# Two of four gate/up units of a 4-bit FFN in three passes of 12-bit digits

## The chip, the cores and the metric

One Trainium2 chip, one NeuronCore of it. TensorE (PE) multiplies matrices, VectorE (DVE), ScalarE (ACT) and GpSimd (POOL) do the element-wise work, and SyncE (SP) issues every DMA of this kernel. Each engine runs its own instructions strictly in the order in which the program lists them, and they meet only in semaphores. The metric is device time in microseconds of one execution.

## The reference

The kernel computes four residual blocks on x of shape (2, 512, 256), each as x + layernorm(block(layernorm(x))):

```python
x = x + ln(softmax_attention(ln(x)))   # 16 heads of 128, rope, causal
x = x + ln(ffn4(ln(x)))                # 4-bit weights, hidden size 2048
x = x + ln(linear_attention(ln(x)))    # elu+1 features, cumulative sums
x = x + ln(ffn_lut(ln(x)))             # 16-entry table, hidden size 688

# ffn4; Wg, Wu, Wd = 4-bit codes -> LUT value * scale per 32 inputs
gate = einsum('th,nh->tn', xt, Wg)     # (1024,256) x (2048,256)
up   = einsum('th,nh->tn', xt, Wu)
gelu = tanh(0.79788 * (gate + 0.044715 * gate**3)) * gate * 0.5 + gate * 0.5
out  = einsum('tn,hn->th', gelu * up, Wd)
```

Everything is float32.

## The kernel before

The 1024 tokens are handled in four units u = 0 to 3 of 256 tokens (two units for each batch row). The program first runs the softmax attention of both rows in 34 slots, one for each of 32 (row, head) pairs and two to drain. Loads of weights, the expansion of the 4-bit codes (`dequantised`, L791, one of twelve jobs in every second slot) and the expansion of the 16-entry table weights of the last FFN are spread over the slots.

After attention come the four units of the 4-bit FFN. `ffn_hidden(u)` (L1089) makes eight steps, one for each pair of 128-row chunks of the hidden size. A step does eight products of 128 x 128 weights with 256 token columns: four for gate into a PSUM bank "mm", four for up into a bank "s" (two banks of each exist). ACT applies gelu to the gate bank (`ge`), DVE multiplies it with the up bank into `hT`. `ffn_out(u)` (L1117) then does 32 products of `hT` with the down weights into a bank "o". The outer loop (L1529 to L1534) runs what is left of hidden(u), then the first step of hidden(u+1), and then ffn_out(u). `hT` has two buffers, "hT" for even units and "hTb" for odd ones, so the first `hT` product of unit u+1 is made ahead of ffn_out(u).

When ffn_out(u) is done, a chain begins (`after_ffn`, L1134): the layer norms (`norms`, L411: statistics and scaled additions on DVE, powers on POOL, shifts on ACT, a block transpose on DVE with four DMAs), then `linear_attention(u)` (L1331: three projections on PE, Relu and Exp on ACT, running sums, products and reciprocals on DVE and POOL), then norms again. Its pieces are dealt out between the PE steps of the next unit. The last FFN follows: `silu_hidden(u)` and `silu_out(u)` for the four units.

A product goes through `matmul` (L277). From L1296 on `halved[0]` is true, and each 128 x 128 weight tile is issued as two tiles of 64 columns; the first few products of the program are issued whole. A float32 product shows two instruction records in the trace for each tile.

The order is written by a planner inside the program. `Engine` wraps DVE, ACT, POOL and SP, keeps an estimate of when each engine is free, and records each instruction at once (all show the line L183). Chains are polled after each PE step and advance when their estimated time has come. `select_in` (L469) turns table indices into weights in 19 DVE steps for each piece; the steps are kept in a queue of fills, and `fill` (L134) puts one ahead of another DVE instruction if it fits before that one's estimated start. `vector.flush()` puts all that are left at once. The down weights `wd` of the last FFN are made in this way from L1323 on, during the FFN units. The order on each engine is then fixed; a wrong estimate cannot change it when it runs.

Of the kernel before, what the change touches and what calls it, by code (L numbers as in the profile page):

```python
# [11 lines left out]
I32 = mybir.dt.int32  # L12
F8 = mybir.dt.float8e4
U8 = mybir.dt.uint8
SIGN = 0x80808080 - (1 << 32)
# [4 lines left out]
P = 128  # L20
HALF = P // 2
B = 2
S = 512
# [167 lines left out]
def sandwich_kernel(  # L191
# [85 lines left out]
    def matmul(out, lhsT, rhs, start, stop, beside=False, **more):  # L277
# [8 lines left out]
        times.add("PE", now[0], [out], [lhsT, rhs])  # L286

    def transpose(out, in_):
        nc.tensor.transpose(out, in_, ident)  # L289
        now[0] = max(now[0], times.start("PE", [out], [in_])) + 0.11  # L290
        times.add("PE", now[0], [out], [in_])
# [13 lines left out]
    sync.dma_start(out=cols_sb, in_=cols)  # L305
    cos_sb = const.tile([P, S], F32, name="cos_sb")
    sin_sb = const.tile([P, S], F32, name="sin_sb")
    bo_sb = const.tile([P, D], F32, name="bo_sb")
    lut_sb = const.tile([P, 16], F32, name="lut_sb")
# [223 lines left out]
    with ExitStack() as at:  # L533
# [4 lines left out]
        ac = at.enter_context(tc.tile_pool(name="ac", bufs=1))  # L538
        dq = at.enter_context(tc.tile_pool(name="dq", bufs=1))

        wts = {}
# [249 lines left out]
        def dequantised(packed, scales, u, name, w):  # L791
# [40 lines left out]

            def values():
                vector.scalar_tensor_tensor(
                    w,
                    c8.bitcast(F8),
                    64.0,
                    sc.unsqueeze(1).to_broadcast([P, 2, UNIT]),
                    ALU.mult,
                    ALU.mult,  # L840
                )

            behind.extend([lambda: scalar.copy(p8, pk), bits, values])

        jobs = deque()
        for u in range(NU):
            for src, sc, name, to in ((gate_p, gate_s, "g", wg_u), (up_p, up_s, "u", wu_u)):
                w = fw.tile([P, 2, UNIT], F32, name=f"w{name}{u}")
                jobs.append((src, sc, u, name, w))
                to.append(w)  # L850
# [224 lines left out]
        def after_attention(b):  # L1075
            yield 0.5
            for u in (2 * b, 2 * b + 1):
                xT1[u] = late.get("lw", acts).tile(
                    TURNED, F32, tag="xT1", name=f"xT1_{u}", bufs=2
                )  # L1080

                y = [half(acc, u)[:, j, :] for j in range(HT)]
                yield from norms(u, y, 1, xT1[u], strided=True)
            holder[0] = None


        hT1 = {}

        def ffn_hidden(u):  # L1089
            if u % 2 == 0:  # L1090
                hT1[u] = fh.tile([P, MLP // P, TU], F32, tag="hT", name=f"hT_{u}", bufs=1)
            else:
                hT1[u] = late["lw"].tile([P, MLP // P, TU], F32, tag="hTb", name=f"hT_{u}")
            nc_u = UNIT // P
            for c2 in range(0, MLP // P, 2):
                pg, pu = bank("mm"), bank("s")
                for ps, ws in ((pg, wg_u), (pu, wu_u)):
                    if ps is pu:
                        yield
                    for j in range(2):  # L1100
                        q, r = divmod(c2 + j, nc_u)
                        for kc in range(NK):
                            matmul(
                                ps[:, j * TU : (j + 1) * TU],
                                ws[q][:, kc, r * P : (r + 1) * P],
                                chunk(xT1[u], kc),
                                kc == 0,
# [9 lines left out]
        def ffn_out(u):  # L1117
            po = bank("o")
            for t in range(HT):
                for c in range(MLP // P):  # L1120
# [7 lines left out]
                    )  # L1128
                    if c % 2 and (t, c) != (HT - 1, MLP // P - 1):
                        yield  # L1130
            begin(after_ffn(u, po))
# [177 lines left out]

    lw = late["lw"] = ctx.enter_context(tc.tile_pool(name="lw", bufs=1))  # L1310
    lp = late["lp"] = ctx.enter_context(tc.tile_pool(name="lp", bufs=2))
    gp = ctx.enter_context(tc.tile_pool(name="gp", bufs=2))
# [7 lines left out]
    carry = {}  # L1320
    scratch = lw.tile([P, 8, 2 * D], F32, name="scratch2")
    vector.flush()
    select_in(  # L1323
        [scratch[:, j] for j in range(8)],
        [
            tuple(t[:, o : o + 2, :].rearrange("p o d -> p (o d)") for t in (down_i, wd))
            for o in range(0, NO, 2)
        ],
    )

    def linear_attention(u):  # L1331
# [22 lines left out]
        for part, e, f in ((1, ek, k), (0, eq, q)):  # L1354
            ps = project(part, "mm")
            scalar.activation(flat(e), ps, AF.Relu, scale=-1.0)
# [6 lines left out]
            else:  # L1363
                yield until(f)
        ps = project(2, "s")
        scalar.copy(flat(v), ps)
# [7 lines left out]
        yield until(k, v)  # L1374
        ks, kvs, den, lT = of("ks", 2), of("kvs", 2), of("den"), of("lT")

        def running_sum(to, of_):
            for ch in range(NK):
                before = carry[to is kvs, u - 1][:, ch, TU - 1 :] if u % 2 else 0.0
                vector.tensor_tensor_scan(  # L1380
                    to[:, ch, :], ones, of_[:, ch, :], before, ALU.mult, ALU.add
                )
            carry[to is kvs, u] = to

# [36 lines left out]

    hT2 = [lw.tile([P, NO, TU], F32, name=f"hT2_{j}") for j in range(2)]
    for t in hT2:
        pool.memset(t[:, FULL, :], 0.0)

    def silu_hidden(u):
# [12 lines left out]
        for o in range(0, NO, 2):  # L1439
            pg, pu = bank("mm"), bank("s")  # L1440
            for j in range(2):
# [7 lines left out]
                else:  # L1449
                    product(pg, at, wg, slice(FULL * P, FULL * P + 64 + REST))  # L1450
            si = gp.tile([P, 2 * TU], F32, tag="si", name="si")
            if o + 1 < FULL:
# [76 lines left out]
    for u in range(NUNIT):  # L1529
        run(hidden)  # L1530
        if u + 1 < NUNIT:
            hidden = ffn_hidden(u + 1)
            run(hidden, 2)
        run(ffn_out(u))  # L1534
    hidden = None
    vector.flush()
    for u in range(NUNIT):
        while u not in xT3:
# [100 lines left out]
```

## Time and profile before

| | |
|---|---|
| median of 3 runs | 618.06 us (617.79 to 618.41) |
| profiled execution, its span from first to last instruction | 616.7 us |
| the median less that span (start and end, outside the profile) | 1.4 us |
| PE busy | 611.1 us, 99% of the span |
| DVE, ACT, POOL busy | 486.2, 309.3, 277.1 us |
| attention, and what is hung on its slots, ends at about | 380 us |
| ffn_out of units 0, 1, 2, 3 begins at about | 390, 437, 486, 531 us |

A line of a group reads: source line, engine, operation, written tile <- read tiles, shapes, count | busy time in us, mean ns of one | idle time of the engine just before, and what ended it. A line of the timeline reads: start in us, duration in us, engine, line, operation, tiles, count; in brackets the idle time before it and what ended that. Shapes such as 128*64 128x256 on PE mean a weight tile of 128 rows and 64 columns, and 256 moving columns. The duration of a PE record contains its pipeline; the pace of PE is read from starts.

### The profile page before, as it was taken

The page shows a single profiled execution, that of the slowest core. Times are in us where ns is not written, and L with a number is a line of the kernel's source. Part 1 is how long each engine was busy: PE and PEld are TensorE (multiplying, and loading weights), DVE is VectorE, ACT ScalarE, POOL GpSimd, SP SyncE. Part 2 cuts the span into 40 slices and gives each one's busy share as a digit, 9 for nine tenths or more (in the row PEclk, how much of TensorE's full clock was granted, in tenths as well). Part 3 has the DMA queues.
Part 4 walks back from the last instruction along what each step waited for, and adds up shares of the span by engine and source line. Part 5 has one row for each costly group of instructions (what it writes and reads, how often), then busy time and mean ns, then how long its engine had stood idle before and what let it go on. Part 6 is the DMA issues. An engine that isn't in the chain of part 4 may idle for free.

```text
span 616.7 us, 13347 instructions
## 1 busy us (share of the span) xinstructions
PE 611.1 (99%) x4968; PEld 470.2 (76%) x4968; DVE 486.2 (79%) x1169; ACT 309.3 (50%) x716; POOL 277.1 (45%) x346
## 2 busy tenths in 40 slices
PE   9999999999999999999999999999999999999996
PEld 7455556566676776767777899999999999996665
DVE  7989988887887999989899789869986751562963
ACT  6657776775666657676566651232324223325210
POOL 5355657454453575855667300350261350161531
PEclk9999999999999999999999999999999999999999
DMA  8477474765647547556552340211001000001010
GB/s 228 137 186 211 107 199 125 171 168 144 158 127 177 168 116 191 152 142 178 113 141 60 84 104 26 98 35 35 1 8 31 1 18 18 1 2 35 19 53 18
DMA packets 44463, 61.43 MB, mean 100 GB/s; under 512 B 5232, under 2 KB 32368, under 8 KB 44400
## 3 DMA queue, kind: packets, MB, share of 16 engines
q1 hardware_dynamic: 44400, 60.59, 38.0%
q8 instruction: 39, 0.64, 0.4%
q14 instruction: 24, 0.20, 0.1%
HBM read 28.59 MB, written 1.05 MB: 48 GB/s over the span
## 4 chain that ended last, share of the span: by engine, by line
PE 98%; DVE 1%; issue 0%; POOL 0%; DVEq 0%
PE ps_mm L282 40%; PE ps_o L282 22%; PE ps_s L282 21%; PE ps_t L282 14%; PE ps_o L579 1%; DVE x L183 0%; DVE p L183 0%; DVE rr L183 0%; DVE ra L183 0%; DVE centred L183 0%; POOL rstd L183 0%; DVE wg L183 0%; PE ps_t L289 0%; DVE st L183 0%; DVE st_last L183 0%
## 5 line engine op out<-in xcount | busy, mean ns | idle before, releaser
L183 DVE SCALAR_TENSOR_TENSOR rr<-ps_mm,cols_sb,sin_sb 64x512 f32<-64x512 f32 (+1 forms) x126 | 93.4, 741 | 3.6 <-PE ps_mm L282 0.7
L183 POOL TENSOR_TENSOR wg<-wg,scratch 128x752 f32<-128x752 f32 x30 | 53.8, 1794 | 89.3 <-DVE scratch L183 86.9
L282 PE MATMUL ps_mm<-xT,wg 128*64 128x256 f32 (+1 forms) x704 | 89.4, 379 | 0.0
L282 PE MATMUL ps_s<-xT,wu 128*64 128x256 f32 x672 | 85.4, 379 | 0.0
L183 ACT ACTIVATE p<-p,mn 128x512 f32<-128x512 f32 (+3 forms) x128 | 70.3, 550 | 27.6 <-DVE mn L183 27.6
L282 PE MATMUL ps_o<-wd,hT 128*64 128x256 f32 (+1 forms) x704 | 77.2, 375 | 0.0
L282 PE MATMUL ps_t<-pT,v 128*64 128x256 f32 (+3 forms) x512 | 76.1, 432 | 0.0
L282 PEld LDWEIGHTS ps_mm<-xT,wg 128*64 128x64 f32 (+1 forms) x704 | 71.7, 137 | 5.5 <-ACT si L183 0.4
L282 PEld LDWEIGHTS ps_o<-wd,hT 128*64 128x64 f32 x704 | 68.9, 137 | 6.2
L282 PEld LDWEIGHTS ps_s<-xT,wu 128*64 128x64 f32 x672 | 69.5, 137 | 4.5 <-DVE hT L183 0.3
L282 PEld LDWEIGHTS ps_t<-pT,v 128*64 128x64 f32 x512 | 49.7, 137 | 27.1 <-issue 19.0
L183 ACT ACTIVATE p<-p,rs 128x512 f32<-128x512 f32 (+3 forms) x128 | 61.4, 551 | 11.2 <-DVE rs L183 9.3
L282 PEld LDWEIGHTS ps_o<-wo,oT 128*64 128x64 f32 x512 | 49.9, 137 | 17.8 <-issue 13.3
L282 PE MATMUL ps_o<-wo,oT 128*64 128x256 f32 x512 | 62.5, 379 | 0.0
L282 PE MATMUL ps_mm<-xT,wq 128*64 128x512 f32 (+2 forms) x256 | 60.5, 577 | 0.1
L282 PE MATMUL ps_mm<-xT,wk 128*64 128x512 f32 x248 | 60.0, 592 | 0.0
L183 POOL TENSOR_TENSOR ra<-ra,cos_sb 128x512 f32<-128x512 f32 (+1 forms) x33 | 41.1, 1245 | 40.2 <-ACT ra L183 38.4
L282 PE MATMUL ps_s<-kT,qT 128*64 128x64 f32 (+5 forms) x384 | 57.0, 424 | 0.0
L282 PE MATMUL ps_mm<-wv,xTv 128*64 128x256 f32 x464 | 56.4, 379 | 0.0
L183 DVE STREAM_TRANSPOSE turned<-p 128x512 f32<-128x512 f32 (+3 forms) x128 | 54.1, 480 | 1.2 <-ACT p L183 0.2
L183 ACT ACTIVATE ln<-x,shift,rstd 128x256 f32<-128x256 f32 x22 | 13.3, 607 | 79.0 <-POOL shift L183 78.2
L282 PEld LDWEIGHTS ps_s<-kT,qT 128*64 128x64 f32 x384 | 34.6, 137 | 23.9 <-issue 11.6
(161 smaller groups left out, 965.3 us busy)
## 6 DMA issues: line engine op xcount, KB each, us to landing
pT<-turned SPq DMA_DIRECT2D x128, 208.0 KB, 3.9
wo<-in_wo SPq DMA_DIRECT2D x17, 256.0 KB, 4.2
wv<-in_wv SPq DMA_DIRECT2D x16, 256.0 KB, 4.2
wq<-in_wq SPq DMA_DIRECT2D x15, 256.0 KB, 4.2
wk<-in_wk SPq DMA_DIRECT2D x15, 256.0 KB, 4.0
xT<-tr SPq DMA_DIRECT2D x48, 64.0 KB, 2.1
pk_g<-in_gate_p SPq DMA_DIRECT2D x4, 256.0 KB, 4.6
sc_g<-in_gate_s SPq DMA_DIRECT2D x8, 128.0 KB, 4.2
```

The costliest lines, as they stand in the source:

```text
L183: return write(*args, **more)
L282: nc.tensor.matmul(out[part], lhsT=lhsT[:, part], rhs=rhs, start=start, stop=stop, **more)
L579: nc.tensor.matmul(warm[:, :P], lhsT=units, rhs=units, start=True, stop=True)
```

## The change

The gate and up products of units 2 and 3 are done on numbers of type float32r, split into parts of 12 bits. A weight w has a top part (its upper bits, by a bit mask), and w = top + the rest; a token x is split alike. A product then takes three passes: weights as they are with tokens as they are, `low` with `low`, `dif` with `dif`, where `low` and `dif` are sums and differences of the parts scaled by powers of 4096. Between the second and the third pass ACT multiplies the PSUM bank by 1 + 1/4096 in place.

What this adds or moves, by place:

- `ffn_hidden_in_digits` takes the place of `ffn_hidden` for units 1 to 3. It is a pipeline: passes 1 and 2 of the next pair are issued ahead of pass 3 of this one. Unit 1 keeps float32 products in it, units 2 and 3 use digits.
- `split_weights` cuts one 128 x 512 piece of gate or up weights: a mask on DVE, a subtraction on POOL (`low`), and at the next call a scaling on ACT and a second subtraction on POOL (`dif`). There are 16 pieces and two buffers for the masked part. It is called after each step of units 1 to 3 and three times in each half of ffn_out(u), u > 0, once the norms of the second row are through. With the first piece of the last quarter it also calls `vector.flush()`.
- `split_tokens` makes the two extra token tiles of units 2 and 3: three DVE operations and one on ACT.
- `hT` has one buffer for all units, so no `hT` product of unit u+1 can stand ahead of ffn_out(u).
- `halved[0]` becomes false after attention, so that all products of the rest are issued whole.
- The expanded gate and up weights go to a staging tile `wt` and are copied into place by a DMA of 512 KB, eight in all, during attention.
- Linear attention projects into banks "t" in place of "mm" and "s", keeps its carries in small tiles, and writes over its inputs where it had own tiles before. Several constants and `hT2` share room with other tiles.

```diff
@@ new helper
+    def digits(out, lhsT, rhs, first):
+        nc.tensor.matmul(out, lhsT=lhsT, rhs=rhs, start=first, stop=False, skip_group_check=True)
+        now[0] = max(now[0], times.start("PE", [out], [lhsT, rhs])) + 0.117
+        times.add("PE", now[0], [out], [lhsT, rhs])
...
@@ dequantised
             def values():
+                to = w if name == "d" else dq.tile([P, 2, UNIT], F32, tag="wt", name=f"wt_{name}{u}")
                 vector.scalar_tensor_tensor(
-                    w,
+                    to,
...
+                if to is not w:
+                    sync.dma_start(out=w.bitcast(F32), in_=to)
...
+        def split_tokens(u):
+            x = xT1[u].bitcast(F32)
+            top = fh.tile(TURNED, F32, tag="ge", name=f"top_{u}")
+            low, dif = (
+                late["lw"].tile(TURNED, F32R, tag=f"x{n}", name=f"x{n}_{u}", bufs=2) for n in ("low", "dif")
+            )
+            vector.tensor_scalar(top.bitcast(I32), x.bitcast(I32), TOP, None, ALU.bitwise_and)
+            vector.scalar_tensor_tensor(dif, top, -1.0 - 1.0 / RADIX, x, ALU.mult, ALU.add)
+            vector.scalar_tensor_tensor(low, dif.bitcast(F32), RADIX, top, ALU.mult, ALU.add)
+            scalar.mul(dif, dif.bitcast(F32), RADIX)
+            x3[u] = xT1[u], low, dif
+
+        def ffn_hidden_in_digits(u):
+            hT1[u] = fh.tile([P, MLP // P, TU], F32, tag="hT", name=f"hT_{u}", bufs=1)
...
+            def begun_(kind, n):
+                ps = banks_of[kind, n] = bank(("mm", "s")[kind])
+                if in_digits(n):
+                    passes(kind, n, (0, 1))
+                    scalar.mul(ps, ps, 1.0 + 1.0 / RADIX)
+                    return
...
+            def ended(kind, n):
+                if in_digits(n):
+                    passes(kind, n, (2,))
+                ps = banks_of.pop((kind, n))
+                if kind == 0:
+                    ge_of[n] = fh.tile([P, 2 * TU], F32, tag="ge", name="ge")
+                    scalar.activation(ge_of[n], ps, AF.Gelu_apprx_tanh)
+                else:
+                    to = hT1[u][:, 2 * n : 2 * n + 2, :].rearrange("p c t -> p (c t)")
+                    vector.tensor_mul(to, ge_of.pop(n), ps)
+
+            for kind in range(2):
+                begun_(kind, 0)
+                yield
+            for n in range(N):
+                for kind in range(2):
+                    ended(kind, n)
+                    if n + 1 < N:
+                        begun_(kind, n + 1)
+                    yield
+                split_weights(1)
+                if n == N // 2 and 1 < u + 1 < NUNIT:
+                    split_tokens(u + 1)
...
@@ ffn_out
                     if c % 2 and (t, c) != (HT - 1, MLP // P - 1):
+                        if c % 6 == 1 and u:
+                            split_weights(1)
                         yield
...
@@ after attention
+    halved[0] = False
...
+    tops = [lw.tile([P, UNIT], F32, name=f"top{j}") for j in range(2)]
+    splits = deque((kind, q, kc) for q in range(NU) for kind in range(2) for kc in range(NK))
+    pending = deque()
+
+    def split_weights(n):
+        for _ in range(n):
+            if holder[0] is not None:
+                return
+            if splits:
+                kind, q, kc = splits.popleft()
+                if (kind, q) not in wl3:
+                    if (kind, q) == (0, NU - 1):
+                        vector.flush()
...
+                top = tops[len(splits) % 2]
+                vector.tensor_scalar(top.bitcast(I32), w.bitcast(I32), TOP, None, ALU.bitwise_and)
+                pool.tensor_sub(low, w, top)
+                pending.append((top, low, dif))
+            if pending and (len(pending) > 1 or not splits):
+                top, low, dif = pending.popleft()
+                scalar.mul(top, top, 1.0 / RADIX)
+                pool.tensor_sub(dif, top, low.bitcast(F32))
...
@@ linear_attention
-            ps = project(part, "mm")
+            ps = project(part, "t")
...
@@ outer loop
-            hidden = ffn_hidden(u + 1)
+            hidden = ffn_hidden_in_digits(u + 1)
```

## Prediction

> **What bounds the kernel now.** I read the page from the top (span, busy time, the 40 slices, the chain), then TensorE's timeline in the FFN units, then the stages in windows, and last the groups of DVE, POOL and ACT whose kind the change adds.
>
> ```profile
> span 616.7 us, 13347 instructions
> PE 611.1 (99%) x4968; PEld 470.2 (76%) x4968; DVE 486.2 (79%) x1169; ACT 309.3 (50%) x716; POOL 277.1 (45%) x346
> PEclk9999999999999999999999999999999999999999
> PE 98%; DVE 1%; issue 0%; POOL 0%; DVEq 0%
> ```
>
> PE never idles, at full clock, and 98% of the chain is PE: taking PE work away shortens the run one for one, as long as nothing else becomes late. The pace of a float32 product is read from the starts of four equal groups in unit 3, each of four 128 x 128 x 256 products:
>
> ```profile
> 509.64 2.00 PE L282 MATMUL ps_s<-xT,wu 128*64 128x256 f32 x16
> 511.37 2.01 PE L282 MATMUL ps_mm<-xT,wg 128*64 128x256 f32 x16
> 513.10 2.01 PE L282 MATMUL ps_s<-xT,wu 128*64 128x256 f32 x16
> 514.82 2.00 PE L282 MATMUL ps_mm<-xT,wg 128*64 128x256 f32 x16
> ```
>
> That is 1.727 us for four, 0.432 us a product. At the start the kernel issues a few products whole, which is the form the rest gets now:
>
> ```profile
> 7.48 0.61 PE L282 MATMUL ps_mm<-xT,wq 128*128 128x128 f32 x4
> 7.93 0.60 PE L282 MATMUL ps_o<-xT,wk 128*128 128x256 f32 x2
> 8.36 0.40 PE L289 MATMUL ps_t<-ident,n 128*128 128x128 f32 x2
> ```
>
> Four records of 128 columns take 0.45 us, 0.112 each; a whole product of 256 columns (two records) takes 0.43.
>
> What hides the other engines' work is ffn_out. Busy time of PE, PEld, DVE, ACT and POOL in ffn_out(1) and in unit 2's other steps:
>
> ```profile
> 437.00:451.00 14.00, 14.00 (x133) 14.00 (x131) 12.67 (x22) 0.72 (x2) 5.33 (x5) 1.00 0.01 2
> 451.00:488.00 37.00, 37.00 (x346) 36.92 (x344) 25.74 (x55) 14.79 (x25) 13.19 (x28) 1.00 0.07 16
> ```
>
> DVE is 90% busy under ffn_out(1), with the select steps of the last FFN's down weights and with linear attention. It can be: the `hT` products on both sides, which PE needs to get on, start 18 us apart (439.91 to 457.89 in the timeline).
>
> The rows for the added and moved work:
>
> ```profile
> L183 DVE TENSOR_SCALAR scratch<-scratch,differ,lut_sb 128x512 int32<-128x512 int32 x21 | 10.7, 537 | 0.1
> L183 DVE COPY_PREDICATED scratch<-scratch 128x512 int32<-128x512 int32 x12 | 9.0, 748 | 0.3
> L183 DVE TENSOR_SCALAR scratch<-scratch 128x512 int32<-128x512 int32 x12 | 4.8, 405 | 0.0
> L183 POOL TENSOR_TENSOR qT<-ra,rr 128x512 f32<-128x512 f32 x32 | 40.9, 1279 | 5.4 <-DVE rr L183 2.8 <-PE ps_s L282 2.6
> L183 ACT ACTIVATE ge<-ps_mm 128x512 f32<-128x512 f32 x32 | 18.8, 593 | 28.9 <-PE ps_mm L282 28.8
> ```
>
> **The change part by part.**
>
> 1. Products removed from PE. Units 2 and 3 have 64 gate and up products each, 128 in all, three passes each instead of 0.432 us. The trace has no float32r pass. From below a pass costs a quarter of a float32 product, 0.108; from above one record of 256 columns, half a product, 0.216. The nearest row is the 0.112 record: the same 128 x 128 weight tile, and streaming of equal length if a float32r column takes half as long as a float32 one. The program's planner counts 0.117. I take 0.115: 3 x 0.115 = 0.345, saving 0.087 x 128 = **-11.1 us**. Ends: -13.8, and +27.6 at 0.216.
>
> The Trainium skill (FP8 and Floating Point Precision, TensorE Precision Notes) says that true FP32 takes four passes and that reduced FP32 is truncated to about 22 bits. Read as one pass against four, that makes the saving a quarter, 13.8 us instead of 11.1. No run here shows it yet.
>
> 2. All other products whole instead of halved: about 408 float32 products stand behind the switch (16 + 64 hidden, 128 out, 64 linear attention, 136 in the last FFN). By 0.43 against 0.432 they cost nothing; two digits of a timeline leave up to 0.005 each, 0 to +2 us. I take **+1**.
>
> 3. Weights cut into digits, 16 pieces. Each is a DVE mask (0.42 by the row of `ek<-ek`, a float tile of the same size), two POOL subtractions (1.28 each) and an ACT scaling (about 0.56, between the 0.50 and 0.72 of its neighbours). POOL gets 32 x 1.28 = 41 us, where it was busy 13 of 37 us in the window above. With two buffers a mask waits for the subtraction two pieces back, so POOL idles for the mask and two hand-overs: about 0.42 + 2 x 1.28 + 0.1 = 3.1 us a piece.
>
> In the changed kernel's order the first calls fall on the last steps of unit 1 (before that the second row's norms hold them off): five masks there, seven under ffn_out(1), four in unit 2. When ffn_out(1) begins POOL has the two sums of linear attention ahead of the seven: 2 x 1.28 + 6 x 3.1 + 1.28 = 22.4 us from the first sum until ACT is released. ACT executes in order, and the gelu of unit 2's first pair and the correction of its second are queued behind the last of these scalings: 0.56 + 0.59 + 0.60 = 1.8 us. PE has until then the last 1.7 us of unit 1, ffn_out(1) with 32 x 0.434 = 13.9, and 24 passes = 2.8: together 18.4. It stands for 22.4 + 1.8 - 18.4 = **+5.8 us**. Ends 2 and 9 us, as the sums begin 2 us sooner (PE further behind) or each subtraction takes 0.1 us longer, some 1.5 us more.
>
> Weighed against that: in the trace the sum `k<-k,ek` beside DVE's copies takes 1.95 us at 441.06 where its twin at 442.97 takes 1.27. The skill (SBUF — State Buffer, two separate sides) says why: DVE and GpSimd share a port pair as "an exclusive lock, not a bandwidth split". If every second one of the 32 subtractions met it at that row's price, POOL would need 16 x 0.68 = 11 us more, part of it in this stall.
>
> 4. The flush. With the 13th piece, after the first `hT` product of unit 2, `flush` lists all that is left of the select steps: between the first and the second `hT` product of unit 2 the changed kernel's DVE has 4 index masks x 0.405, 8 pairs x 0.537, 8 picks x 0.748 (11.9 us), the piece's mask 0.42, two scans 2 x 0.68 (`kvs`), a carry copy (0.2, an estimate from the 0.18 of a 2-column aggregate), a reciprocal 0.9 and the product 0.69: 15.5, less some 0.5 for starts that overlap by 0.05 to 0.1 us. With two "s" banks PE can do 24 more passes, 2.8 us, before the up products of the fourth pair need the bank that this second product frees: **+12.2 us**. Before, such a stretch lay under ffn_out; now `hT` has one buffer, the first product stands behind ffn_out(1), and that cover of 14 us is gone. Ends 10 and 13.5 (PE three or more groups further back or none).
>
> 5. ACT around Exp in unit 1. From the end of the last projection ACT does a copy 0.59, a table load 1.28, two Exp 0.63 + 0.62, now also two scalings of digits 2 x 0.56, a table load 1.28 and the gelu 0.59: 6.1 us. PE has two groups, 3.5 us. Before, ffn_out stood next; now another step of unit 1 does: **+2.6**, ends 0 and 4.
>
> 6. The rest of units 2 and 3. A third pass needs ACT's correction, which has the 1.4 us of 12 other passes as cover where gelu had 3.5. What lies on ACT and DVE between (norms, the token split with 0.42 + 2 x 0.76 on DVE before ACT's scaling, the last pieces) comes out above that in about two places by 2 to 3 us each, with small ones beside: **+6**, ends 2 and 9.
>
> 7. The end. The products of the last unit's linear attention go two PE groups earlier into silu_out(1), and the norms behind them stand ahead of the silu products of unit 2 on DVE: 0 to 2.5, **+2**.
>
> 8. At nothing: the eight 512 KB copies. Each waits for its DVE step and is issued behind the slot's four `pT` DMAs; behind it in SP's queue stand the loads of v and o for two slots on, and the next `pT` comes 11 us later. Attention's DMA share is 0.40 to 0.70, `pT` lands in 3.9 us, so 5 to 6 us for a copy fits in the slot. Without that cover one copy could hold a slot for 2 us; 0 to +4 for all. The moved constants, small carries and banks "t": -1 to +1, 0.
>
> Sum: -11.1 + 1 + 5.8 + 12.2 + 2.6 + 6 + 2 = +18.5 us on the profiled span of 616.7, so 635.2. With the 1.4 us that lie around it and no other difference to the median of 618.06: **636.6 us**, 1.030 times the time before.
>
> **The rivals.**
>
> - Faster: the digits give what PE saves. For it speaks 99% PE; against it DVE's 90% under ffn_out(1) and the place of the flush. It needs the stalls of steps 3 to 7 to stay under 10.1 us together; the flush alone decides it, at 15 us of DVE work against 2.8 us of PE work. With the flush hidden and the rest at the low ends (4 us) the time is 618.1 - 10.1 + 4 = 612. Chance 0.05.
> - Half of it: the flush costs its 12 us, POOL and ACT keep up, the others at 2 to 3 us: 618.1 - 10.1 + 15 = 623. For it: an idle POOL under ffn_out(1) before (5.3 of 14 us). Chance 0.10.
> - POOL is the bound: subtractions stretched by the shared port (1.95 against 1.27) add 5 to 9 us to steps 3 and 6: 643. Chance 0.19.
> - A digit pass is no faster than a float32 record (0.216): +27.6 instead of -11.1, while the slower PE hides some 15 us of the stalls: 618.1 + 27.6 + 1 + 14 = 661. Against it: the planner's 0.117. Chance 0.04.
>
> **How the numbers follow.** My case has 0.62 (630 to 641 by its own ends). The range leaves out the faster case, most of "half of it" and the slow pass, 0.17 in all: 627 to 646. Below 0.2% (1.2 us) two times of this kernel can't be told apart. Faster 0.05 and a little of "half of it": 0.06; same 0.01; slower 0.93.
>
> **What will show it.** Starts of the digit groups of four 0.45 to 0.47 us apart (step 1); PE idle about 12 us between the second and third pair of unit 2 with DVE in unbroken select steps (4); idle PE at the end of ffn_out(1) with ACT waiting for POOL (3); about 2.6 us in the last steps of unit 1 behind a table load (5). I am wrong if DVE has done the select steps earlier, if POOL's 128 x 512 subtraction is well under 1.28 us, or if digit passes start more than 0.13 us apart.

## The result, and the profile after

The changed kernel takes 649.62 us (median, 648.66 to 650.62) against 617.92 us of the kernel before (617.74 to 618.41): 1.051 times the time, interval 1.0496 to 1.0526. Forecast were 636.6 us and a range to 646. The profiled execution, itself 648.94 us, has a span of 647.2 us where it was 616.7: 30.5 more. The direction was right, the size was not.

The page of the changed kernel, its span, busy times, clock row and chain:

```profile
span 647.2 us, 11583 instructions
PE 610.8 (94%) x4028; PEld 435.8 (67%) x4028; DVE 511.1 (79%) x1195; ACT 336.1 (52%) x766; POOL 325.0 (50%) x378
PEclk9999999999999999999999999999778899999999
PE 74%; DVE 13%; POOL 7%; issue 2%; DMA 2%; ACT 1%; SPq 1%; POOLq 0%; DVEq 0%
```

PE is 94% busy instead of 99%, and DVE and POOL now hold a fifth of the chain. The clock row is new: two 7s and two 8s, where before there were only 9s. Busy PE is no smaller, although its products are cheaper: part of them ran at half clock (6.2 us more, see the table below).

TensorE's timeline shows the three long waits (start, duration, what; in brackets the idle time and what ended it):

```profile
468.19 1.22 PE L297 MATMUL ps_mm<-xdif,wl 128*128 128x256 f32 x4 [10.98 <-ACT ps_mm L190]
...
487.30 1.22 PE L297 MATMUL ps_s<-xT,wu 128*128 128x256 f32 x4 [11.35 <-DVE hT L190]
...
503.83 0.76 PE L297 MATMUL ps_mm<-xdif,wl 128*128 128x256 f32 x4 [2.90 <-ACT ps_mm L190]
```

The first is the end of ffn_out(1) (step 3), the second the flush (step 4), the third the cutting of unit 3's tokens (step 6), behind which ACT had the gelu and the correction:

```profile
502.18 0.63 ACT L190 ACTIVATE xdif<-xdif 128x512 fp32r<-128x512 f32 x1 [2.35 <-DVE xlow L190]
```

The first wait ends with ACT's work in its order, behind the last of the scalings that had to wait for POOL. The first line is the first of the two sums of linear attention, with which the sum of step 3 begins:

```profile
439.91 1.26 POOL L190 TENSOR_TENSOR k<-k,ek 128x512 f32<-128x512 f32 x1
...
466.47 1.71 POOL L190 TENSOR_TENSOR wl<-top,wl 128x512 fp32r<-128x512 f32 x1
466.54 0.63 ACT L190 ACTIVATE top<-top 128x512 f32<-128x512 f32 x1 [2.96 <-POOL wl L190]
467.07 0.58 ACT L190 ACTIVATE ge<-ps_mm 128x512 f32<-128x512 f32 x1
467.55 0.59 ACT L190 ACTIVATE ps_mm<-ps_mm 128x512 f32<-128x512 f32 x1
```

From 439.91 until ACT is released at 466.54 POOL takes 26.6 us; step 3 had 22.4. TensorE ends its last group at 457.2, 17.3 us behind the first sum; step 3 had 18.4.

Measured as lost time (from one start to the next, less the pace of the products) the three waits are 11.0, 11.4 and 3.0 us; 2.8 and 0.5 us around 434 us (step 5) and 2.3 us before 623.0 us (step 7) complete the list.

The digit groups of four, at full clock and, behind the first wait, at half clock:

```profile
455.13 0.64 PE L297 MATMUL ps_mm<-xlow,wl 128*128 128x256 f32 x4
455.61 0.65 PE L297 MATMUL ps_s<-xdif,wl 128*128 128x256 f32 x4
...
470.06 1.05 PE L297 MATMUL ps_mm<-xlow,wl 128*128 128x256 f32 x4
470.92 1.05 PE L297 MATMUL ps_s<-xdif,wl 128*128 128x256 f32 x4
471.77 1.05 PE L297 MATMUL ps_s<-xT,wu 128*128 128x256 f32 x4
```

At full clock they start 0.48 us apart, 0.120 a pass; then 0.85 apart, 0.214 a pass. Stretches of the changed kernel show it in the clock column (busy PE, PEld, DVE, ACT, POOL, then the mean granted clock):

```profile
468.20:475.90 7.70, 7.70 (x40) 7.54 (x40) 7.55 (x16) 2.70 (x5) 6.64 (x8) 0.60 0.01 3
475.90:487.30 11.40, 0.05 (x1) 0.00 (x0) 11.16 (x18) 1.60 (x3) 4.96 (x5) 0.73 0.00 0
487.30:491.20 3.90, 3.90 (x18) 3.90 (x19) 3.76 (x10) 1.66 (x3) 3.30 (x5) 0.50 0.00 0
```

In the middle row PE does nothing and DVE is busy for 11.16 of 11.40 us: that is the flush. Groups that answer to the cost rows of before:

```profile
L190 DVE TENSOR_SCALAR scratch<-scratch,differ,lut_sb 128x512 int32<-128x512 int32 x21 | 14.3, 716 | 0.1
L190 POOL TENSOR_TENSOR wl<-top,wl 128x512 fp32r<-128x512 f32 x16 | 23.1, 1445 | 7.6 <-ACT top L190 7.6
L190 POOL TENSOR_TENSOR wl<-wg,top 128x512 fp32r<-128x512 f32 x8 | 12.3, 1544 | 11.8 <-DVE top L190 8.8 <-DMA xT<-tr 3.1
L190 ACT ACTIVATE top<-top 128x512 f32<-128x512 f32 x16 | 10.1, 630 | 38.9 <-POOL wl L190 38.9
```

The same 21 select steps that took 537 ns before take 716, the subtractions of these two rows take 1445 and 1544 where 1280 was taken, and ACT waited 38.9 us for POOL.

The terms, as forecast and as this profile has them:

| step | forecast | measured |
|---|---|---|
| 1 products (128 x 0.432 less 384 passes) | -11.1 | -9.2 (0.120 a pass) |
| 2 whole products | +1 | 0 (an ffn_out of 13.81 us from start to next start, before and after) |
| 3 stall at the end of ffn_out(1) | +5.8 | 11.0 |
| 4 flush | +12.2 | 11.4 |
| 5 ACT around Exp | +2.6 | 3.2 |
| 6 rest of units 2, 3 | +6 | 3.0 |
| 7 the end | +2 | 2.3 |
| 8 copies | 0 | 0.9 (three late `pT`, 0.17 + 0.30 + 0.38) |
| half clock | none | 6.2 (66 passes x 0.094) |
| the rest, by subtraction (no wait over 0.3 us is left in it) | none | 1.7 |
| sum on the span | +18.5 | +30.5 |

### The profile page after: what moved, and what is told of

Same layout as the page of the kernel before. It is cut to its first block, busy times and chain, and to the rows that moved or that the text cites. A ratio compares the mean times of both kernels' runs of the same rounds, so it can differ in the third digit from the quotient of the medians.

```text
span 647.2 us, 11583 instructions
## 1 busy us (share of the span) xinstructions
PE 610.8 (94%) x4028; PEld 435.8 (67%) x4028; DVE 511.1 (79%) x1195; ACT 336.1 (52%) x766; POOL 325.0 (50%) x378
## 3 DMA queue, kind: packets, MB, share of 16 engines
HBM read 28.59 MB, written 1.05 MB: 46 GB/s over the span
## 4 chain that ended last, share of the span: by engine, by line
PE 74%; DVE 13%; POOL 7%; issue 2%; DMA 2%; ACT 1%; SPq 1%; POOLq 0%; DVEq 0%
PE ps_mm L289 26%; PE ps_o L289 16%; PE ps_t L289 15%; PE ps_s L289 12%; POOL wl L190 4%; DVE scratch L190 3%; PE ps_s L297 2%; PE ps_mm L297 2%; DMA pT<-turned 2%; DVE wd L190 1%; POOL rstd L190 1%; DVE top L190 1%; DVE hT L190 1%; POOL shift L190 1%; DVE xTv L190 1%
## 5 line engine op out<-in xcount | busy, mean ns | idle before, releaser
L289 PE MATMUL ps_o<-wd,hT 128*128 128x256 f32 (+1 forms) x352 | 76.9, 376 | 2.1 <-DVE x L190 2.1
L289 PEld LDWEIGHTS ps_o<-wd,hT 128*128 128x128 f32 x352 | 65.8, 190 | 11.1 <-DVE x L190 2.5
L289 PEld LDWEIGHTS ps_t<-pT,v 128*64 128x64 f32 x512 | 41.2, 137 | 36.5 <-issue 27.3
L289 PEld LDWEIGHTS ps_o<-wo,oT 128*64 128x64 f32 x512 | 41.9, 137 | 25.7 <-issue 15.3
L289 PE MATMUL ps_mm<-xT,wg 128*128 128x256 f32 (+2 forms) x280 | 55.2, 380 | 2.6 <-ACT ge L190 2.6
L289 PE MATMUL ps_s<-kT,qT 128*64 128x320 f32 (+5 forms) x384 | 57.2, 424 | 0.0
L289 PE MATMUL ps_s<-xT,wu 128*128 128x256 f32 (+1 forms) x264 | 51.3, 380 | 0.3 <-DVE hT L190 0.3
L190 DVE CUSTOM_DVE_ANT_0 p<-ps_s,mask 128x512 f32<-128x512 f32 x64 | 31.2, 488 | 25.7 <-PE ps_s L289 21.6
L289 PEld LDWEIGHTS ps_mm<-xT,wg 128*128 128x128 f32 (+2 forms) x280 | 42.2, 168 | 8.9 <-ACT ge L190 3.0
L190 POOL TENSOR_TENSOR rstd<-ve,mhalf 128x1 f32<-128x1 f32 (+1 forms) x65 | 40.6, 626 | 11.2 <-DVE ve L190 6.0
```

What stands on the lines that cost most here:

```text
L190: return write(*args, **more)
L289: nc.tensor.matmul(out[part], lhsT=lhsT[:, part], rhs=rhs, start=start, stop=stop, **more)
```

## The experiments

**Theory A**: the digits give what PE's pace promises, and the time is lost in waits for cutting the weights (ACT behind POOL, DVE in the flush) and in the clock that falls while PE waits. **Rival B**: the new layout, the single `hT` above all, costs most. **Rival C**: the passes themselves bring the clock down. **Rival D**, on the stall of step 3: DVE and POOL slow each other, and that, not the hand-overs, made it twice the forecast.

### The layout without digits

```diff
             def in_digits(n):
-                return u > 1
+                return False
...
-                if n == N // 2 and 1 < u + 1 < NUNIT:
-                    split_tokens(u + 1)
...
     def split_weights(n):
+        return
```

> The changed kernel with all its layout (one hT buffer, whole products, the pipeline over pairs, the staged copies, shared tiles) but with float32 products in all units: no cutting of weights or tokens, no flush. Theory A (the loss is the cutting's waits, the flush and what follows them): what stays against 617.9 is attention's late pT (+0.9 in the gaps of TensorE), a gelu behind Exp in unit 1 (+1.5 to 2.8) and the stall before the last ffn_out (+2.3), so 622 to 625, full clock after the start. Theory B (the layout costs most of it, above all the single hT): 635 or more, with TensorE idle at the end of each ffn_out.

Measured: 625.9 us (618.2 before; ratio 1.0126, 1.0111 to 1.0141), as A said up to 1 us, and far from B's 635. PE's waits are 1.76 us twice behind gelu and Exp (units 1 and 2), 2.3 at the end, and 1 us of late `pT`: 6.8 of the 7.7 us. The layout is a real cost, a quarter of the loss. Step 5's two terms come apart as well: 1.76 without the scalings of digits, 2.78 with two of them in the changed kernel; the difference, 1.0, is about their 2 x 0.56.

### The digits with their cutting left out

```diff
-                        w = (wg_u, wu_u)[kind][q] if k == 0 else wl3[kind, q][k - 1]
+                        w = (wg_u, wu_u)[kind][q]
...
     def split_weights(n):
+        return
```

> The changed kernel with the cutting of the weights left out: passes two and three read the weights as they are, so the output is not the reference's; no pieces on DVE, POOL and ACT and no flush. TensorE does exactly the passes of the changed kernel. Theory A: 9.2 us less than the layout alone (128 products at 0.36 instead of 0.432), plus about 1 for the cutting of the tokens: 614 to 618; groups of four passes 0.48 us apart throughout, granted clock full. Rival C (passes of this type themselves bring the clock down): intervals at half clock in units 2 and 3 although no stall is there, groups 0.85 apart in them, 622 or more.

Measured: 617.1 us, ratio 0.9991 (0.9979 to 1.0003). That is 8.8 less than the layout alone, for the 9.2 expected less the tokens' cutting. The granted clock is full until the last 1 us of the span (only 9s in the clock row of its page), so rival C falls: 384 passes as such don't lower it. And the ceiling of the change in this layout is seen: with the cutting for nothing, the kernel only draws level with before. The other 32.5 us belong to cutting the weights, with the flush that this calls and the half clock behind the stalls.

### No flush

```diff
             def in_digits(n):
-                return u > 1
+                return u > 1 and 2 * n < (NU - 1) * (UNIT // P)
...
-    splits = deque((kind, q, kc) for q in range(NU) for kind in range(2) for kc in range(NK))
+    splits = deque((kind, q, kc) for q in range(NU - 1) for kind in range(2) for kc in range(NK))
```

> The last quarter of the gate and up products of units 2 and 3 (pairs 7 and 8) stays in float32, so its four pieces are not cut and the flush is not called; the other 12 pieces as before. Theory A: the stall of 11.4 us before the fourth pair of unit 2 goes with about 1.7 us of half clock behind it; 32 products cost 0.072 more each, +2.3; the stall of 11.0 at the end of ffn_out(1) stays, since the same seven pieces lie there: 636 to 641. Rival (the select steps that the flush put there only move to another place where DVE is late): a new stall before some other hT product, 645 or more.

Measured: 630.2 us (ratio 1.0197, 1.0182 to 1.0212), 19.5 less than the changed kernel and 6 to 11 better than expected. The flush's stall is gone, with 0.6 us in its place; the stall of step 3 stands, 1.1 us shorter:

```profile
467.64 1.22 PE L297 MATMUL ps_mm<-xdif,wl 128*128 128x256 f32 x4 [9.92 <-ACT ps_mm L190]
...
477.75 0.75 PE L297 MATMUL ps_s<-xT,wu 128*128 128x256 f32 x4 [0.54 <-DVE hT L190]
```

What made it better than the flush's 11.4, on the spans (647.2 to 628.3, 18.9): with the new order the third stall and the one at the end went too (3.0 - 0.6 and 2.3), 1.1 of the first, and of the 6.2 us of half clock all but about 1.5, with 1.7 new behind a stall that ends at 433.7; attention was 0.6 quicker; the 32 float32 products gave 2.3 back. 11.4 + 2.4 + 2.3 + 1.1 + 3.0 + 0.6 - 2.3 = 18.5. So the flush itself is 11.4, the length of its stall in the changed kernel. How much of the rest hung on it, and how much comes from the other order that the program writes here, this run does not show.

### The second subtraction on DVE

```diff
-                scalar.mul(top, top, 1.0 / RADIX)
-                pool.tensor_sub(dif, top, low.bitcast(F32))
+                vector.scalar_tensor_tensor(dif, top, 1.0 / RADIX, low.bitcast(F32), ALU.mult, ALU.subtract)
```

> The scaling on ACT and the second subtraction on POOL of each piece become one operation on DVE (top/4096 - low, some 0.75 us by the rows of that kind). Theory A (ACT, which executes in order, holds the gelu and the correction back behind scalings that wait for POOL): the stall at the end of ffn_out(1) falls from 11.0 to 4 or less with some 2 us of half clock; DVE has 16 x 0.75 more, a part of it before hT products: stall of the flush 12 to 14 instead of 11.4; 639 to 645. Rival D (DVE and POOL slow each other, and their sum sets the pace): the pieces stay over 3 us apart, the stall over 8, the time 647 or more.

Measured: 650.3 us, no gain. ACT's wait is gone, but a wait for DVE took its place, and the flush became longer:

```profile
465.24 1.22 PE L297 MATMUL ps_s<-xT,wu 128*128 128x256 f32 x4 [7.26 <-DVE hT L190]
...
484.51 1.22 PE L297 MATMUL ps_s<-xT,wu 128*128 128x256 f32 x4 [12.48 <-DVE hT L190]
```

A missed: the mechanism of its first half is right (no ACT in the way any more), its price is not. Of rival D the time came (647 or more), but not its stall of over 8 us. DVE had no room: in this order 31 select steps were left for the flush instead of 20, since the added operations took the places in which they had been put.

### Without the select steps

```diff
-    select_in(
-        [t[:, j, :] for t in last_q for j in range(2 * NK)],
-        [
-            tuple(t[:, o : o + 2, :].rearrange("p o d -> p (o d)") for t in (down_i, wd))
-            for o in range(0, NO, 2)
-        ],
-    )
+    for o in range(0, NO, 2):
+        sync.dma_start(out=wd[:, o : o + 2, :].bitcast(I32), in_=down_i[:, o : o + 2, :])
```

> The table lookup of the last FFN's down weights is left out (the indices are loaded in their place, so the output is not the reference's): the 57 select steps of DVE, among them the flush, are gone; all 16 pieces are cut as before. Both theories take the flush's stall away (without it e3_no_flush came to 630, with 2.3 us of float32 products in it: 628). Theory D (POOL's subtractions were stretched by DVE's work beside them): they fall from 1.45 to about 1.3 us, pieces under ffn_out(1) come 3.1 us apart, the stall at its end falls from 11 to 5 to 7: 621 to 625. Rival (the order of ACT, DVE and POOL in each piece sets the pace, with or without the select steps): subtractions of 1.4 and more, a stall of 9 to 11, 626 to 631.

Measured: 635.3 us (ratio 1.0285, 1.0270 to 1.0301). The stall of step 3, and the subtractions in it where DVE has nothing to do:

```profile
456.98 1.27 POOL L190 TENSOR_TENSOR wl<-wg,top 128x512 fp32r<-128x512 f32 x1 [0.54 <-DVE top L190]
458.21 1.27 POOL L190 TENSOR_TENSOR wl<-top,wl 128x512 fp32r<-128x512 f32 x1
...
460.02 1.26 POOL L190 TENSOR_TENSOR wl<-wu,top 128x512 fp32r<-128x512 f32 x1 [0.54 <-DVE top L190]
461.24 1.27 POOL L190 TENSOR_TENSOR wl<-top,wl 128x512 fp32r<-128x512 f32 x1
...
462.97 1.23 PE L297 MATMUL ps_mm<-xdif,wl 128*128 128x256 f32 x4 [5.36 <-ACT ps_mm L190]
```

The same stretch of the changed kernel:

```profile
457.41 1.64 POOL L190 TENSOR_TENSOR wl<-wg,top 128x512 fp32r<-128x512 f32 x1 [0.54 <-DVE top L190]
457.96 1.37 DVE L190 TENSOR_SCALAR ek<-ek 128x512 f32<-128x512 f32 x1
459.01 1.44 POOL L190 TENSOR_TENSOR wl<-top,wl 128x512 fp32r<-128x512 f32 x1
...
461.26 1.94 DVE L190 TENSOR_SCALAR scratch<-scratch,differ,lut_sb 128x512 int32<-128x512 int32 x2
461.42 1.50 POOL L190 TENSOR_TENSOR wl<-wg,top 128x512 fp32r<-128x512 f32 x1 [0.97 <-DVE top L190]
```

Rival D is borne out for the pace: beside idle DVE a subtraction takes 1.27 and a piece 3.04 us. In the changed kernel, beside select steps and DVE's part of linear attention, most subtractions of these pieces take 1.38 to 1.77, DVE's `ek<-ek` takes 1.37 instead of 0.42, and the pieces come 3.7 us apart on average.

For the stall it explains half. From the first sum until ACT is released POOL takes 23.9 us here (437.42 to 461.31) and 26.6 in the changed kernel, which is 2.7 of the 5.6 us between the two stalls. The other 2.9 are TensorE's place: the first sum begins 3.3 us before ffn_out(1) here and 0.5 in the changed kernel, since no select steps stand ahead of the masks on DVE and since TensorE in this run was at half clock from 434.72 to 438.13. So this stall of 5.4 does not confirm the 5.8 that had been forecast.

The Trainium skill (SBUF — State Buffer, SBUF: two separate sides) states that the port pair of DVE and GpSimd is an exclusive lock, taken by some DVE operations only (those with two SBUF inputs or in a two-port mode); both engines lengthening in these lines agrees with it, without any line that shows the port itself. A busy DVE alone does not slow POOL: in the kernel before, DVE was busy for 94% of the time of the 32 operations `qT<-ra,rr`, mostly with block transposes and with operations that read PSUM, and each of the 32 took 1.27 to 1.30 us.

The time missed its 621 to 625: new waits of 3.1 us for DVE before 469.6 and of 2.7 us later in unit 2, the 2.3 us at the end, which stayed, and four stretches at half clock.

### PE kept busy in the two stalls

```diff
+            def warm(n):
+                ps = bank("t")
+                for _ in range(n):
+                    digits(ps[:, :TU], wg_u[0][:, 0, :P], chunk(x3[u][0], 0), True)
...
+                if (u, kind, n) == (2, 1, 3):
+                    warm(84)
...
+                if (u, kind, n) == (2, 0, 0):
+                    warm(84)
```

> The changed kernel with 84 passes more on TensorE in each of the two long stalls (into a PSUM bank that nobody reads; 10.1 us at full clock, the stalls are 11.0 and 11.4). Theory A (the clock was halved because TensorE had idled): the granted clock stays full through both stalls and the groups behind them are 0.48 us apart. The first recovery, some 2.6 us, is given back at the second stall, whose end is set by DVE's select steps; the 1.7 us behind the second stall are kept, as far as the third stall leaves them: 646.5 to 648.5. Rival C (passes of this type or the load bring the clock down): intervals at half clock stay, 649.5 or more.

Measured: 654.1 us. The clock stayed full through both filled stalls, and the groups behind them are 0.48 us apart; behind a new stall of 3.6 us that was not filled it fell to a half. The time says nothing on the price, since the program's planner had counted the added passes and moved other engines' work. So once more, with the passes outside the planning and 110 of them in the second stall:

> As e6_warm, but the added passes (84 before the first stalled group, 110 before the second) are kept out of the program's planning, so that DVE, ACT, POOL and SP have exactly the order of the changed kernel (in e6_warm the planner counted them and moved other engines' work). Theory A (idling halves the clock): full clock through both stalls and behind them; the first stall ends at the same time, the second too (DVE's select steps set it, so the 2.6 us won behind the first are waited away), and only what was lost behind the second stall and the third is kept, 1.7 to 3 us of 649.6: 646.5 to 648.5. Rival (the passes themselves bring the clock down): half clock behind the stalls, 649.5 or more.

Measured: 649.7 us, equal to the changed kernel. Stretches of this kernel in the two stalls and behind them, to be read against those of the changed kernel above:

```profile
454.70:468.20 13.50, 13.49 (x111) 13.25 (x110) 9.99 (x12) 3.67 (x7) 11.32 (x8) 1.00 0.00 1
473.60:487.40 13.80, 13.38 (x112) 13.17 (x110) 13.52 (x22) 1.60 (x3) 7.00 (x7) 1.00 0.00 1
487.40:512.00 24.60, 19.89 (x144) 18.66 (x145) 16.23 (x35) 13.87 (x27) 17.56 (x29) 1.00 0.06 14
```

Clock 1.00 throughout: idling lowers it, and filling the idle time keeps it. But the second stall, now from 473.6 to 487.4, is 13.8 us and ends where it ended before: DVE sets its end, and what PE won it waited. Of 6.2 us of half clock 1.2 were won by 512 us, and two other short stalls, which end at 433.9 and 621.8, cost a stretch of half clock each that they had not cost in the changed kernel's profile. The expected 646.5 to 648.5 was too good; the mechanism is shown, its net price in this kernel, by the 1.2 us won by 512 us, is about 1 us, and the time of this run shows none of it.

### The layout without the copies

The edits of the first experiment, and these:

```diff
-                to = w if name == "d" else dq.tile([P, 2, UNIT], F32, tag="wt", name=f"wt_{name}{u}")
+                to = w
...
-                if to is not w:
-                    sync.dma_start(out=w.bitcast(F32), in_=to)
```

> As e1_layout_only, but the expanded gate and up weights are written in place by DVE, without the staging tile and the eight 512 KB copies. If the copies make pT late in attention (gaps of 0.17, 0.30 and 0.38 us of TensorE before products with pT, which the kernel before does not have): 0.8 to 1.1 us less than that run, 624.8 to 625.2, and the gaps are gone. If the gaps come from something else in the layout: no difference, 625.6 to 626.2.

Measured: 626.35 us in the median (624.75 to 626.57), so by the time no gain. By the profile the gaps before products with `pT` are gone, and PE is 1.0 us earlier up to the last ffn_out. There it loses it again, to the clock. The stall at the end (2.1 us idle, 2.3 from start to start), in the layout with copies and then in this one:

```profile
599.86 4.58 PE L289 MATMUL ps_o<-wd,hT 128*128 128x256 f32 x20 [2.12 <-DVE x L190]
```

```profile
598.78 6.27 PE L289 MATMUL ps_o<-wd,hT 128*128 128x256 f32 x20 [2.11 <-DVE x L190]
```

The same wait, and behind it the same 20 records in 4.58 or in 6.27 us: here the clock was at half for the 3.41 us from 599.06.

### Both edits, and a smaller change

The edits of the third and fourth experiments together:

> The edits of e3_no_flush (last quarter in float32, no flush) and e4_dif_on_dve (one DVE operation in place of ACT's scaling and POOL's second subtraction) together. Theory A: no flush, and the stall at the end of ffn_out(1) is no longer ACT's; what stays is DVE's lateness there (7.3 us in e4_dif_on_dve, with select steps and the flush behind it): 618 to 627. Rival (DVE has no room left, so its 12 operations more only move the stall): 630 or more.

Measured: 625.5 us (ratio 1.0126, 1.0109 to 1.0143), within what A gave. The wait of 7.3 us for DVE at the end of ffn_out(1) stayed, the flush and what stood behind it did not come.

Then half of the digits, with the cover of ffn_out restored. Only eight pieces are cut, and the second part of each is made on DVE as in the fourth experiment; of the edits these are the new ones:

```diff
             def in_digits(n):
-                return u > 1
+                return u > 1 and 2 * n < 2 * (UNIT // P)
...
-            hT1[u] = fh.tile([P, MLP // P, TU], F32, tag="hT", name=f"hT_{u}", bufs=1)
+            hT1[u] = (fh if u % 2 == 0 else late["lw"]).tile([P, MLP // P, TU], F32, tag="hT" if u % 2 == 0 else "hTb", name=f"hT_{u}", bufs=1)
...
-        yield until(lT) - 0.8 if last else until(lT) + 0.5
+        yield until(lT) + 1.0 if last else until(lT) + 0.5
...
-            run(hidden, 2)
+            run(hidden, 4)
```

> Digits for the first half of the gate and up products of units 2 and 3 only (pairs 1 to 4, eight pieces to cut, no flush), each piece's second part by one DVE operation, the second hT buffer back and four steps of the next unit (so its first hT product) ahead of ffn_out, and the last out-projection of linear attention 1.8 us later in the plan. By the terms: 64 products x 0.072 = 4.6 us less, late pT in attention +0.9, gelu behind Exp under the cover of ffn_out 0, end 0, remaining waits on DVE 0.5 to 3: 614.5 to 617.5 against 618. If DVE's 8 masks, 8 operations and the cutting of the tokens make hT products late even so: 620 or more.

> As e11_two_quarters, with the expanded gate and up weights written in place by DVE as float32r instead of through the staging tile and eight DMA copies. If the late pT of attention comes from the copies: 0.8 to 1.1 us less than e11_two_quarters, 613.5 to 616.5. If not: the same as that run.

Measured: 619.26 us (ratio 1.0021, 1.0012 to 1.0030) with the copies and 617.57 us (0.9992, 0.9984 to 1.0001) without. The copies cost 1.7 us here (1.1 in the profiled spans); both are 1 to 2 us above their expectations. What the second one still waits for in the last steps of unit 1:

```profile
436.21 0.75 PE L297 MATMUL ps_s<-xT,wu 128*128 128x256 f32 x4 [1.28 <-DVE hT L190]
...
439.99 0.62 PE L297 MATMUL ps_s<-xdif,wl 128*128 128x256 f32 x3 [0.99 <-DVE wl L190]
```

> As e12_two_quarters_no_copies, but the first pair of unit 2 stays in float32: there TensorE still waited 1.34 us for a late hT product of unit 1 and 1.05 us for a piece of digits. If those two waits come from TensorE reaching the pair too early for DVE (eight products of 0.36 in a place where DVE has select steps, pieces and the sums of linear attention): 0.6 us more of TensorE work, up to 2.4 us less waiting, 615.7 to 617.0. If DVE is simply late there: the waits move to the next pair, 617.5 to 618.5.

Measured: 617.67 us (0.9992, 0.9983 to 1.0001). The waits moved to the next pair (0.5 and 1.4 us): DVE is late there whoever comes first. No version was found that is faster than before by more than can be measured; two are level with it.

## Why the prediction was wrong in size

- **Step 1**, a term too good by 1.9: a pass is 0.120 us at full clock, not 0.115; the saving is 9.2. The rival of the slow pass and the ceiling of 13.8 are both out.
- **Step 2** is nothing: ffn_out takes 13.81 us with halved and with whole products.
- **Step 3** is the step that failed: 11.0 us for 5.8. Its chain was right (mask, POOL, ACT in order, gelu and correction behind the last scaling). What it had wrong is the price of a piece, 3.1 us: from the first sum until ACT was released POOL took 26.6 us instead of 22.4. Of these 4.2 us some 3.4 are the subtractions (13 of them, 1.54 us on average instead of 1.28), and about 1 is POOL idle for masks that came late on DVE. Another 1.1 us is TensorE, done 17.3 us behind the first sum instead of 18.4. The forecast took 1.28 us from a row beside which DVE does other operations, and gave the slower row (1.95 against 1.27), the one beside a select step, to a rival; under ffn_out(1) the slower kind was the normal case. That the run without select steps has a stall of 5.4 is luck: POOL takes 23.9 us there, and TensorE is done only 20.2 us behind the first sum. The rival "POOL is the bound" had this mechanism and 0.19; with its 643 us it came nearest.
- **Step 4** came to 11.4 for 12.2, by two errors that cancel. DVE's stretch from one `hT` product to the next was 17.0 us, not 15.0 (the carry copy took 1.05 instead of 0.2, the two scans 2.3 instead of 1.4, both beside a subtraction on POOL); and PE filled 5.6 us of it instead of 2.8, mainly because it ran at half clock. At full clock, in the second of the two runs that kept PE busy, the stall is 13.8, above the term's own upper end.
- **Step 5** (3.2 for 2.6) and **step 7** (2.3 for 2) held. **Step 6** was too dear, 3.0 for 6: of the two places that it named one came, the cutting of unit 3's tokens, at the price named.
- **Step 8** was not free: the copies make `pT` late three times. In this profile that is 0.9 us, and 1.7 in the time of the two smaller changes, which differ in nothing else; in the two layouts the clock took the gain back.
- **No term** stood for the clock, although the forecast had PE idle for 12.2 us in one place and 5.8 in another. It is 6.2 us gross. Since the next stall took most of it back, about 1 us is its own; in a kernel that goes on at PE's pace behind a stall it would be all of it (no run here is such a kernel).
- The 12.0 us between the forecast and the measured span are 5.2 of step 3, 6.2 of the clock, 1.9 of step 1, 0.9 of step 8, 0.6 and 0.3 of steps 5 and 7 and 1.7 of the rest, less 1 of step 2, 0.8 of step 4 and 3 of step 6.
- The range ended at 646 because the clock had no bound in it and the slower subtraction of step 3 was put into a rival instead of into the range's upper end.

## What to carry to other kernels

A duration is taken from the row whose neighbours do the same operations as they will after the change; that they are busy is not enough. On POOL an operation of 128 x 512 took 1.28 us beside DVE's transposes and mostly 1.38 to 1.77 beside its select steps and scans, and DVE's part grew by more. Moving work to an engine that is 90% busy moves the stall with it; count first what the change costs with its extra work for free (here: a draw), and drop it if that is no gain. A stall of TensorE is priced with the clock behind it, and then one asks whether the next stall takes that back.

## What the runs showed of the hardware

- The granted clock changes at multiples of 3.41 us on a grid of its own. In the changed kernel it was at half from 460.72 to 474.37 (4 x 3.41), from 481.19 to 491.44 (3 x) and from 505.09 to 508.50 (1 x). It came back only at the end of a stretch of the grid in which PE had been busy almost throughout: after the restart at 468.19 the stretch to 470.95, busy for 0.81, did not release it, the next one did. The lowest busy share behind which it came back in these traces was 0.92 (run without select steps, 489.33 to 492.74).
- Idle time shorter than one such stretch can be enough: 2.6 us of idle PE before 433.7 halved it in the run without the flush, and so did 2.1 us at the end in the layout without copies, while the same 2.1 us in the layout with copies and 2.6 us in the changed kernel did not. What differs is how the idle time falls on the grid (first line: the run without the flush; the other two: the changed kernel):

```profile
430.41:433.82 3.41, 0.78 (x5) 0.35 (x4) 3.38 (x6) 3.39 (x6) 1.33 (x1) 1.00 0.25 77
...
430.00:433.41 3.41, 1.70 (x8) 1.14 (x6) 3.38 (x5) 3.39 (x6) 1.29 (x1) 1.00 0.19 63
433.41:436.83 3.42, 2.22 (x9) 1.66 (x10) 3.39 (x9) 1.84 (x4) 0.00 (x0) 1.00 0.04 14
```

In the run without the flush (first line) PE was busy for 0.23 of one stretch, and the clock fell; in the changed kernel the same stall lay across two, busy for 0.50 and 0.65, and it did not. The two layouts differ likewise: 2.1 us idle in one stretch (busy for 0.38), or 1.0 and 1.1 in two (0.71 and 0.67). The highest busy share at which it fell in these traces was 0.44 (456.37 to 459.79, both edits together), the lowest at which it did not was 0.45 (621.14 to 624.55, changed kernel). The Trainium skill (TensorE: Matmul & The Clock Gate, Part 1, What's actually happening) gives a free-running window of 3413 ns, which these times agree with, and lets the clock fall after at least one idle window; here a window that was idle for 0.56 of its time did it, so a rule of full idle windows is too lenient.

- A product of 128 x 128 by 256 columns in float32r starts every 0.120 us, in float32 every 0.432; three such passes are five sixths of the float32 product.
- On this kernel's DVE and POOL, some 128 x 512 operations lengthen each other: `ek<-ek` on DVE took 0.42 us alone and 1.37 beside a subtraction, a subtraction 1.27 alone and up to 1.77. Beside DVE's transposes and operations that read PSUM, POOL stayed at 1.27 to 1.30.
